# Convolution, attention and expert layers in one launch: a second convolution's split, copies and bursts moved between VectorE, ScalarE and GpSimd

## The chip, the core and the metric

The kernel runs on one core of one Trainium2 chip. A core has five engines that run side by side, each in the order of its own instruction stream: TensorE (PE; its weight loads are listed apart as PEld), VectorE (DVE), ScalarE (ACT), GpSimd (POOL) and SyncE (SP), which here only issues DMAs. They wait for each other through semaphores. The metric is the device time of one launch in microseconds (us), the median of several runs; lower is better.

## The reference

The input is x, 8 images of 56 x 56 positions with 256 channels, float32. Two layers follow each other:

```
# layer 0: 32 narrow paths, each 256 -> 4 -> 4 (3x3) -> 256, summed
h = relu(bn(x @ w1 + b1))            # per path, D = 4
h = relu(bn(conv3x3(h, w2) + b2))
h = relu(bn(h @ w3 + b3))
x = relu(paths.sum(axis=0) + x)
# layer 1: linear attention over an image's tokens, then experts
t = tokens(x)                                    # (8, 3136, 256)
q = ln(t); k = layernorm_per_head(q); v = layernorm_per_head(q)   # 8 heads of 32
kv = einsum('bhnd,bhne->bhde', k, v) / N
t = t + (einsum('bhnd,bhde->bhne', q, kv) + q)
u = ln(t); top2 = top_k(softmax(u @ router_w.T), 2)
t = t + (u + sum over the two experts of weight * expert(u))   # gelu(u @ w1 + b1) @ w2 + b2
```

The layer norms of the heads use the unbiased standard deviation plus 1e-5. The weights of the two experts are normed to the sum 1.

## The kernel before

**Chunks and slots.** The tokens are cut into S = 56 chunks of 448 tokens (CH), seven for each image. The main loop (L1395) runs over slots s = 0 to 64. A slot holds work on several chunks at once: the third convolution of chunk s (`conv3_steps`), the first of chunk s + 2, the second of chunk s + 1, the attention sums of chunk s - 1 (`end_steps`), the attention output of chunk s - 8 (`attn_steps`), the routing of one or two earlier chunks (`route_steps`), the planning of expert tiles (`plan_steps`), and expert tiles of 256 rows (`moe_steps`). Slots 0 to 8 have convolutions and sums alone, later ones attention too, then experts; the slots after 56 have no convolution, and the last expert tiles run by themselves.

**Order.** Every kind of work is a list of steps, pairs of a cost and a function. `issue` (L1368) lays each list over a stretch of the slot, for instance 0.12 to 1.0 for `end_steps`: a step stands at the middle of its share of the cost, and all steps of the slot are issued by position. The costs are thus only spacing. On PE, ACT and DVE this order is the engine's order; POOL and SP get theirs from a scheduler at build time, and it is fixed as well.

**Third convolution.** `pair` (L577) is the pulse of the kernel: two matmuls into two PSUM tiles (L587), a ReLU on ACT from the first into `r` (L592), and one DVE instruction that takes the maximum of the second and adds `r` (L595). A chunk has 32 pairs. After each four, `sum_paths` (L601) adds the four `r` with matmuls (L608). PSUM has seven working tiles, `r` seven buffers.

**Second convolution.** `conv2_steps` (L289) makes 24 small matmuls in three steps; ACT writes `h2` (L306). The next step, `halves` (L309), splits it for the products of pairs: DVE rounds `h2` to `hi` (L314) and takes the rest, `lo` (L315), and SP spreads both with 16 DMAs of 56 KB into `hl` (L320), in four groups (`ab`) of hi, lo, hi, lo. The first four pairs of the next slot read group 0, the next four group 1, and so on.

**Sums for the heads.** In `end_steps`: DVE sums each head's 32 channels (`means`, L667) and scales the result (L670), POOL subtracts it from the tokens (`center`, L681), ACT squares (L690), DVE works out the variances in one step (L699 to L718), POOL raises 36 numbers a partition to the power 0.5 (L719), DVE inverts (`inverse`, L727 to L733), POOL multiplies (L737), PE makes the products (L747).

**Attention, routing, experts.** `attend` (L866) has two matmuls, an update of X on DVE (L874) and statistics (L881, L882); after the fourth, POOL takes a power -0.5 of four numbers a partition (L885), and `means` (L887) uses it on DVE (L889) and `normed` on ACT (L894). `rows` (L1011) writes the two weights and the token's number behind the 256 values of each row of `pay` (L1019 to L1021); POOL scatters the rows to a region in DRAM (L1031). `take_rows` loads 256 of them into `z` (tag "rows", four buffers), `take_weights` an expert's weights (L1234, four buffers). `tile_in` (L1239) turns `z` and copies its weights to `g` (L1252) and its numbers to `index` (L1256); `tile_out` (L1295) scales the product by `g` on ACT (L1311), and POOL adds the result into the output by a scatter (L1325).

Of the kernel before, what the change touches and what calls it, by code (L numbers as in the profile page):

```python
# [8 lines left out]
F32 = mybir.dt.float32  # L9
BF16 = mybir.dt.bfloat16  # L10
I32 = mybir.dt.int32
F32R = mybir.dt.float32r
# [13 lines left out]
def kernel(  # L26
# [24 lines left out]
    nc = tc.nc  # L51
# [174 lines left out]
    nc.gpsimd.memset(h1[:, 1 : HW + 1, HW + 1 : W58], 0.0)  # L226

    def is_chunk(s):
        return 0 <= s < S
# [59 lines left out]
    def conv2_steps(s):  # L289
        ps = []  # L290

        def taps_of(dy):
            if dy == 0:
                ps.append(ps_mm.tile([P, 512], F32, tag="mm", name=f"c2_{s}"))
            R = tapped[s]
            for g in range(NG):
                nc.tensor.matmul(  # L297
                    ps[0][32 * g : 32 * g + 32, :CH],
                    W2t[:, g, dy, :],
                    R[:, g, :].rearrange("q (r w) -> q r w", w=W58)[:, dy : dy + ROWS, :HW],  # L300
                    start=(dy == 0), stop=(dy == 2),
                )
            if dy == 2:
                del tapped[s]
                h2 = split.tile([P, CH], F32, tag="h2", name=f"h2_{s}")
                nc.scalar.activation(h2, ps[0][:, :CH], AF.Relu, bias=sh2, scale=sc2)  # L306
                h2s[s] = h2

        def halves():  # L309

            h2 = h2s[s]
            hi = split.tile([P, CH], F32R, tag="hi", name=f"hi_{s}")
            lo = split.tile([P, CH], F32R, tag="lo", name=f"lo_{s}")
            nc.vector.tensor_copy(hi, h2)  # L314
            nc.vector.tensor_tensor(lo, h2, hi.bitcast(F32), ALU.subtract)  # L315
            hl = hlp.tile([P, NQ, CH], F32R, tag="hl", name=f"hl_{s}")
            for ab in range(NQ):
                for v, part in enumerate((hi, lo, hi, lo)):
                    queue = nc.scalar if s == 0 and v % 2 else nc.sync
                    queue.dma_start(  # L320
                        out=hl[v : P : 4, ab, :].bitcast(F32),
                        in_=part[32 * ab : 32 * ab + 32, :].bitcast(F32),
                    )
            h2s[s] = hl

        return [
            (0.8, lambda: taps_of(0)), (0.8, lambda: taps_of(1)), (0.8, lambda: taps_of(2)),
            (0.8, halves),
        ]

# [75 lines left out]
    for f in range(NF):  # L406
        tp = ps_mm.tile([P, 512], F32, tag="mm", name=f"tp_sb_{f}")
        nc.tensor.transpose(tp[:, :NP], bias3[:, f * P : (f + 1) * P], ident[:NP, :NP])
        b3T = setup.tile([P, NP], F32, name=f"b3T_{f}")
        nc.scalar.copy(b3T, tp[:, :NP])  # L410
        sub = setup.tile([P, NQ, NPL], F32, name=f"sub_{f}")
        nc.vector.tensor_copy(
            sub, b3T.rearrange("q (a r n) -> q a r n", r=2, n=NPL)[:, :, 1, :]
        )
        nc.vector.tensor_reduce(
            sumb[:, f, :], sub.rearrange("q a n -> q (a n)"), AX.X, ALU.add
        )
    setup_pool.__exit__(None, None, None)

# [65 lines left out]
    Wd = tc.dram_tile([E, P, WROW], F32, name="Wd")  # L485

    b2hl = const.tile([P, C], F32R, name="b2hl")
    b2s = const.tile([P, C], F32, name="b2s")
    b2l = const.tile([E, C], F32R, name="b2l")
    nc.gpsimd.memset(b2s, 0.0)  # L490
    nc.sync.dma_start(out=b2s[:E], in_=b2)
    nc.vector.tensor_copy(b2hl, b2s)
    nc.vector.tensor_tensor(b2l, b2s[:E], b2hl[:E].bitcast(F32), ALU.subtract)
    nc.sync.dma_start(out=b2hl[E : 2 * E].bitcast(F32), in_=b2l.bitcast(F32))
    pos_i = const.tile([P, 2], I32, name="pos_i")
# [9 lines left out]

    ids = const.tile([T, KT], I32, name="ids")
    nc.gpsimd.iota(ids, [[T, KT]], base=0, channel_multiplier=1)
    def tiles_after(n):
# [127 lines left out]
    def end_steps(s):  # L636
# [28 lines left out]
        def means():  # L665
            m = v["m"] = small([T, KT, NH], "hmean")
            nc.vector.tensor_reduce(  # L667
                m, v["t"].rearrange("q k (h c) -> q (k h) c", c=HC), AX.X, ALU.add
            )
            nc.vector.tensor_scalar_mul(m, m, 1.0 / HC)  # L670

# [6 lines left out]

        def center():
            for f, n in enumerate(heads(norm)):  # L680
                nc.gpsimd.tensor_tensor(  # L681
# [13 lines left out]
        def variances():  # L695

            sd = v["sd"] = small([T, KT, NH + 1], "hsd")
            ss = small([T, KT, NH], "hss")
            nc.vector.tensor_reduce(  # L699
                ss, v["sq"].rearrange("q k (h c) -> q (k h) c", c=HC), AX.X, ALU.add  # L700
            )
            m = v["m"]
# [5 lines left out]
                op0=ALU.mult, op1=ALU.add,  # L708
            )
            nc.vector.tensor_mul(dm, dm, dm)  # L710
            nc.vector.scalar_tensor_tensor(
                dm, dm, float(HC), ss, op0=ALU.mult, op1=ALU.add
            )
            nc.vector.tensor_reduce(mu, dm, AX.X, ALU.add)
            nc.vector.tensor_scalar(
# [7 lines left out]
        def inverse():  # L723
# [6 lines left out]
            )  # L730
            nc.vector.reciprocal(inv, inv)
            rs1s[s] = keep.tile([T, KT], F32, tag="rs1", name=f"rs1_{s}")
            nc.vector.reciprocal(rs1s[s], sd[:, :, NH])  # L733
# [8 lines left out]
        def products():  # L742
# [13 lines left out]

        return [
            (0.1, begin), (0.6, lambda: turn(0)), (0.6, lambda: turn(1)), (0.6, means),
            (1.0, center), (0.6, squares), (1.8, variances), (0.8, inverse), (0.8, scale),
            (1.9, products),  # L760
        ]
# [91 lines left out]
    def attn_steps(a):  # L853
# [9 lines left out]
        nm = stat.tile([T, KT], F32, tag="nm", name=f"nm_{a}")  # L863
        late = []

        def attend(k):  # L866
# [10 lines left out]
            )  # L877
            late.append(lambda: nc.scalar.copy(lg[:, k, :], ps[:, C:]))
            if k:
                late.pop(0)()  # L880
            nc.vector.bn_stats(st[:, k, :], X[:, k, :])  # L881
# [5 lines left out]
        def means():  # L887
            late.pop(0)()
            nc.vector.scalar_tensor_tensor(  # L889
                nm, mv[:, :, 0], -1.0, rs2, op0=ALU.mult, op1=ALU.mult  # L890
            )

# [6 lines left out]
        def base():  # L899
# [9 lines left out]

        return (  # L910
            [(1.0, lambda k=k: attend(k)) for k in range(KT)]
            + [(0.6, means)]
            + [(0.4, lambda k=k: normed(k)) for k in range(KT)]
            + [(0.6, base)]
        )
# [11 lines left out]
    def route_steps(group):  # L927
# [10 lines left out]
        def logit():  # L938
            lg = v["lg"] = small([E], "rlg")
            for n, m in enumerate(group):  # L940
# [4 lines left out]
                )  # L945
                nc.vector.tensor_add(mine, mine, raw[:, :, E:])

        dsc = desc[:T, None, :].to_broadcast([T, K, E])

        def wide(t):  # L950
            return t[:, :, None].to_broadcast([T, K, E])

        def best(n):
# [10 lines left out]
            nc.vector.tensor_reduce(mx, lg, AX.X, ALU.max)  # L964
            nc.vector.tensor_tensor(sel, lg, wide(mx), ALU.is_equal)
            nc.vector.tensor_tensor(sel, sel, dsc, ALU.mult)
            nc.vector.tensor_reduce(at, sel, AX.X, ALU.max)
            nc.vector.tensor_tensor(sel, dsc, wide(at), ALU.is_equal)

        def weights():  # L970
            q = v["q"] = small([], "rq")
            nc.vector.tensor_sub(q, v["mx", 1], v["mx", 0])
            for n, m in enumerate(group):
                mine = q[:, n * KT : (n + 1) * KT]
                nc.vector.tensor_mul(mine, mine, pays[m][3])  # L975
            nc.gpsimd.tensor_tensor(q, ebase[:T, :K], q, ALU.pow)  # L976
            both = v["both"] = small([2, E], "rboth", BF16)
            nc.vector.tensor_copy(both, v["sel"])
# [32 lines left out]
        def rows():  # L1011
            q2 = v["q"]
            q1 = small([], "rq1")
            nc.vector.tensor_scalar_add(q1, q2, 1.0)
            nc.vector.reciprocal(q1, q1)
            for n, m in enumerate(group):
                pay = pays[m][0]
                mine = slice(n * KT, (n + 1) * KT)
                nc.vector.tensor_copy(pay[:, :, C], q1[:, mine])  # L1019
                nc.vector.tensor_mul(pay[:, :, C + 1], q2[:, mine], q1[:, mine])  # L1020
                nc.vector.tensor_scalar_add(pay[:, :, C + 2].bitcast(I32), ids, m * CH)  # L1021
            row = small([2], "rrowf")
# [7 lines left out]
        def scatter(n, m, k):  # L1030
# [12 lines left out]

        return [
            (0.5, logit), (0.5, lambda: best(0)), (0.5, lambda: best(1)), (0.5, weights),
            (0.6, ranks), (0.5, rows),
        ], [
# [162 lines left out]
    def empty_rows(e):  # L1210
        pad = slots.tile([P, 2, ROW], F32, tag="rows", name=f"pad_{e}")
        nc.gpsimd.memset(pad, 0.0)
# [7 lines left out]
    def take_rows(i):  # L1220
        row = entry(i, 0, E * CAPR - TR)
        z = slots.tile([P, 2, ROW], F32, tag="rows", name=f"rows_{i}")
        region = regions[slot_of[i][2]]
# [15 lines left out]
    def tile_in(i):  # L1239
# [9 lines left out]
        nc.scalar.copy(eT, tp)  # L1249

        g = slots.tile([P, 2], F32, tag="g", name=f"g_{i}")
        nc.vector.tensor_copy(g, z[:, :, C + k])  # L1252
        index = slots.tile([P, 2], I32, tag="index", name=f"index_{i}", bufs=6)
# [250 lines left out]
```

## Time and profile before

| | |
|---|---|
| median of 3 runs | 3389.59 us (3385.21 to 3398.8) |
| the profiled execution's own time | 3376.6 us |
| its span, first to last instruction | 3374.9 us |
| mean granted TensorE clock | 0.951 |
| PE busy | 3001.6 us, 89% |
| DVE busy | 2179.8 us, 65% |
| ACT busy | 1895.8 us, 56% |
| POOL busy | 1928.4 us, 57% |
| DMA | 537.72 MB, mean 159 GB/s |

Busy time is the time in which an engine executed something. A group of the profile gives line, engine, operation, output <- input, shape and count, and then busy time, mean duration in ns, the engine's idle time just before, and what ended most of it. In the timeline each row has the start, the duration and the instruction; a bracket is the idle time of that engine before it, with the instruction that ended it. Rows that follow each other with equal work are merged, with a count. Executions differ a little: the profiled one lies 13 us under the median.

### The profile page before, as it was taken

The numbers are of one execution on the slowest core, as the hardware profiler recorded it, in microseconds if no ns is written. First come the engines' busy times: TensorE is split into PE (matmuls) and PEld (weight loads), VectorE is DVE, ScalarE is ACT, GpSimd is POOL, SyncE is SP. The second block draws the span as 40 slices with busy tenths as digits, with TensorE's granted clock in tenths as the row PEclk, the third lists the DMA queues.
The fourth block names the chain that finished last, engine by engine and source line by source line (L and its number), as shares of the span: only waits on it lengthen the run. The fifth ranks groups of instructions, "written<-read, shape, count | busy, mean of one in ns | idle before, by whom it ended". The sixth has DMA issues, their size and how long they took to land. (4 is left out here: it accounts for less than half of the span.)

```text
span 3374.9 us, 55166 instructions
## 1 busy us (share of the span) xinstructions
PE 3001.6 (89%) x16677; PEld 1697.5 (50%) x16677; DVE 2179.8 (65%) x5762; ACT 1895.8 (56%) x3799; POOL 1928.4 (57%) x1386
## 2 busy tenths in 40 slices
PE   5888888888898999999999999899989987888698
PEld 2343433443444554555545555455444545676577
DVE  3666777777877777776776777776777774333200
ACT  2656555545565666566655666566656654443345
POOL 2222244444556566657565666746656657777677
PEclk7999989989999999999999999999999999988799
DMA  6432334445466676666666667567665756888797
GB/s 146 121 86 84 91 103 123 120 123 150 129 162 159 164 197 168 166 165 174 175 163 163 159 185 187 148 177 187 158 180 152 187 149 159 201 217 218 173 222 178
DMA packets 341481, 537.72 MB, mean 159 GB/s; under 512 B 59952, under 2 KB 251584, under 8 KB 341184
## 3 DMA queue, kind: packets, MB, share of 16 engines
q1 hardware_dynamic: 257088, 429.93, 43.8%
q0 software_dynamic: 81984, 103.45, 16.9%
q8 instruction: 134, 2.20, 0.3%
q14 instruction: 163, 1.34, 0.1%
q10 hardware_dynamic: 2112, 0.81, 0.1%
HBM read 248.01 MB, written 192.55 MB: 131 GB/s over the span
## 5 line engine op out<-in xcount | busy, mean ns | idle before, releaser
L595 DVE SCALAR_TENSOR_TENSOR r<-c,nb,r 128x448 f32<-128x448 f32 x1792 | 1127.3, 676 | 556.7 <-ACT r L592 482.8
L592 ACT ACTIVATE r<-c,b3t 128x448 f32<-128x448 f32 x1792 | 1033.2, 636 | 359.4 <-PE c L587 338.6
L1325 POOL DMA_INDIRECT out_dram<-y,index x420 | 662.8, 1578 | 356.3 <-ACT y L1311 243.7
L587 PE MATMUL c<-hl,W3hl 64*128 64x448 f32 x3584 | 708.4, 428 | 74.4 <-ACT r L592 37.7
L608 PE MATMUL su<-r,gather 128*32 128x448 f32 x3584 | 574.5, 568 | 64.9 <-DVE r L595 38.4
L1031 POOL DMA_INDIRECT regions<-pay,rrowi x448 | 433.1, 967 | 314.1 <-PE c L587 204.2
L587 PEld LDWEIGHTS c<-hl,W3hl 64*128 64x128 f32 x3584 | 341.9, 188 | 505.6 <-issue 227.1
L1287 PE MATMUL ph<-eT,w 128*128 128x256 f32 x1680 | 468.1, 410 | 55.7 <-DMA w<-Wd 23.8
L1307 PE MATMUL py<-w,hT 128*128 128x256 f32 x1680 | 435.6, 384 | 0.0
L1311 ACT ACTIVATE y<-py,g 128x256 f32<-128x256 f32 x420 | 196.7, 475 | 402.1 <-PE py L1307 303.1
L1287 PEld LDWEIGHTS ph<-eT,w 128*128 128x128 f32 x1680 | 306.9, 198 | 196.9 <-issue 101.8
L719 POOL TENSOR_TENSOR hsd<-hsd,half 112x36 f32<-112x36 f32 x56 | 351.7, 6280 | 78.4 <-DVE hsd L718 77.7
L1291 ACT ACTIVATE hT<-ph,w 128x256 f32<-128x256 f32 x420 | 198.1, 477 | 308.5 <-PE ph L1287 165.6
L1307 PEld LDWEIGHTS py<-w,hT 128*128 128x128 f32 x1680 | 293.9, 193 | 28.7
L681 POOL TENSOR_TENSOR norm<-t,hmean 112x512 f32<-112x512 f32 x112 | 120.2, 1130 | 322.1 <-PE c L587 175.0
L870 PE MATMUL at<-tab,tT 128*112 128x272 f32 x896 | 266.1, 421 | 11.9 <-ACT y L1311 6.8
L608 PEld LDWEIGHTS su<-r,gather 128*32 128x32 f32 x3584 | 104.2, 110 | 272.9 <-issue 135.5
L1303 PE MATMUL py<-b2hl,own 128*128 128x256 f32 x420 | 178.7, 425 | 22.4 <-ACT pay L894 8.1
L870 PEld LDWEIGHTS at<-tab,tT 128*112 128x112 f32 x896 | 149.4, 181 | 92.0 <-issue 17.3
L297 PE MATMUL c<-R,W2t 96*32 96x448 f32 x1344 | 180.1, 567 | 3.9 <-DMA R<-h 3.0
L894 ACT ACTIVATE pay<-X,nm,rs 112x256 f32<-112x256 f32 x224 | 134.9, 603 | 75.1 <-DVE nm L889 64.4
L976 POOL TENSOR_TENSOR rq<-ebase,rq 112x8 f32<-112x8 f32 (+1 forms) x32 | 52.9, 1654 | 197.0 <-DVE rq L975 197.0
(246 smaller groups left out, 3198.5 us busy)
## 6 DMA issues: line engine op xcount, KB each, us to landing
w<-Wd SPq DMA_DIRECT2D x210, 513.0 KB
rows<-regions SPq DMA_DIRECT2D x210, 259.0 KB
xi<-in_x_dram SPq DMA_DIRECT2D x56, 448.0 KB
hl<-hi SPq DMA_DIRECT2D x448, 56.0 KB
tTs<-u SPq DMA_DIRECT2D x56, 448.0 KB
ts<-t SPq DMA_DIRECT2D x56, 448.0 KB
tT<-tTs SPq DMA_DIRECT2D x56, 448.0 KB
X<-ts SPq DMA_DIRECT2D x56, 448.0 KB
```

Source lines behind the costliest of these rows:

```text
L587: product = nc.tensor.matmul(tiles[g][:, :CH], W3hl[rows, ab, cg, :], hl[rows, ab, :], start=True, stop=True)
L592: nc.scalar.activation(r, tiles[0][:, :CH], AF.Relu, bias=b3t[:, cg, 2 * ab : 2 * ab + 1])
L595: nc.vector.scalar_tensor_tensor(r, tiles[1][:, :CH], nb3[:, cg, 2 * ab + 1 : 2 * ab + 2], r, op0=ALU.max, op1=ALU.add,)
L608: nc.tensor.matmul(ps[32 * c4 : 32 * c4 + 32, :CH], gather, unit.pop((s, 4 * u + c4)), start=(ab == 0), stop=(ab == NQ - 1),)
L719: nc.gpsimd.tensor_tensor(sd, sd, half[:T, :].rearrange("q (k h) -> q k h", k=KT), ALU.pow)
L870: nc.tensor.matmul(ps, tT[:, f, k * T : (k + 1) * T], tables_of[b][:, f, :], start=(f == 0), stop=(f == NF - 1),)
L1031: ins = nc.gpsimd.indirect_dma_start(out=regions[n], out_offset=bass.IndirectOffsetOnAxis(ap=v["row_i"][:, (m - group[0]) * KT + k, n : n ...
L1287: nc.tensor.matmul(ps, w[:, f * C + hf * P : f * C + (hf + 1) * P], eT[:, f, :], start=(f == 0), stop=(f == NF - 1),)
L1291: nc.scalar.activation(hT[:, hf, :], ps, AF.Gelu, bias=w[:, 2 * NF * C + hf : 2 * NF * C + hf + 1])
L1307: nc.tensor.matmul(ps, hT[:, f, h * P : (h + 1) * P], w[:, (NF + f) * C : (NF + f + 1) * C], start=False, stop=(f == NF - 1),)
L1311: nc.scalar.activation(y[:, h, :], ps, AF.Identity, scale=g[:, h : h + 1])
L1325: ins = nc.gpsimd.indirect_dma_start(out=out_rows, out_offset=at, in_=y[:, h, :], in_offset=None, compute_op=ALU.add, **partial,).ins
```

## The change

- `conv2_steps`: ACT writes both `h2` and `hi` from PSUM; DVE's rounding copy goes. `lo` is made by POOL instead of DVE.
- `end_steps`: the two large sums over heads are each made in two halves, and the chain of the variances is cut over five steps, that of the inverse over two. `in_parts` runs a function as a generator, one part for each step. The scaling by 1/32 goes from DVE to ACT, at the head of `center`. A step without work, `pause`, of cost 1.7 stands between the power and the inverse, and one of 0.3 behind the inverse; the cost given to the variances goes from 1.8 to 1.2.
- `attn_steps`: each `attend` is cut in two, and pauses stand on both sides of `means`; the token's number is written by an iota on POOL in a step of its own.
- `route_steps`: the steps are cut in parts; `rows` takes the reciprocal straight into `pay`, without copies, and adds no numbers; q + 1 is an instruction with two tensors.
- Expert tiles: `g` is now a view of `z`, so that `z` is held until `tile_out`; `z` has five buffers instead of four.
- The preparation of `b2hl` moves into the setup pool, which frees its memory; `ids` goes.

The core of the diff:

```
+    def in_parts(cost, n, fn):
+        run = []
+        def part(k):
+            if not run:
+                run.append(fn())
+            for _ in run[0]:
+                if k < n - 1:
+                    return
+        return [(cost / n, lambda k=k: part(k)) for k in range(n)]
+    def pause(cost):
+        return (cost, lambda: None)
...
-                nc.scalar.activation(h2, ps[0][:, :CH], AF.Relu, bias=sh2, scale=sc2)
-                h2s[s] = h2
+                hi = split.tile([P, CH], F32R, tag="hi", name=f"hi_{s}")
+                for part in (h2, hi):
+                    nc.scalar.activation(part, ps[0][:, :CH], AF.Relu, bias=sh2, scale=sc2)
+                h2s[s] = (h2, hi)
...
-            nc.vector.tensor_copy(hi, h2)
-            nc.vector.tensor_tensor(lo, h2, hi.bitcast(F32), ALU.subtract)
+            nc.gpsimd.tensor_tensor(lo, h2, hi.bitcast(F32), ALU.subtract)
...
-            nc.vector.tensor_reduce(
-                m, v["t"].rearrange("q k (h c) -> q (k h) c", c=HC), AX.X, ALU.add
-            )
-            nc.vector.tensor_scalar_mul(m, m, 1.0 / HC)
+            for h in range(2):
+                nc.vector.tensor_reduce(
+                    m[:, 2 * h : 2 * h + 2],
+                    v["t"][:, 2 * h : 2 * h + 2].rearrange("q k (h c) -> q k h c", c=HC),
+                    AX.X, ALU.add,
+                )
+                yield
...
         def center():
+            nc.scalar.mul(v["m"], v["m"], 1.0 / HC)
...
-            (0.1, begin), (0.6, lambda: turn(0)), (0.6, lambda: turn(1)), (0.6, means),
-            (1.0, center), (0.6, squares), (1.8, variances), (0.8, inverse), (0.8, scale),
-            (1.9, products),
+            (0.1, begin), (0.6, lambda: turn(0)), (0.6, lambda: turn(1)),
+            *in_parts(0.8, 2, means), (1.0, center), (0.6, squares),
+            *in_parts(1.2, 5, variances), pause(1.7), *in_parts(0.5, 2, inverse), pause(0.3),
+            (0.8, scale), (1.9, products),
...
+        def number():
+            nc.gpsimd.iota(
+                pay[:, :, C + 2].bitcast(I32), [[T, KT]], base=a * CH, channel_multiplier=1
+            )
...
-            [(1.0, lambda k=k: attend(k)) for k in range(KT)]
-            + [(0.6, means)]
+            sum((in_parts(1.0, 2, lambda k=k: attend(k)) for k in range(KT)), [])
+            + [pause(0.6), (0.3, means), pause(0.2)]
             + [(0.4, lambda k=k: normed(k)) for k in range(KT)]
-            + [(0.6, base)]
+            + [(0.1, number), (0.5, base)]
...
-            nc.vector.tensor_scalar_add(q1, q2, 1.0)
-            nc.vector.reciprocal(q1, q1)
+            nc.vector.scalar_tensor_tensor(
+                q1, q2, 1.0, half[:T, :K], op0=ALU.add, op1=ALU.max
+            )
...
-                nc.vector.tensor_copy(pay[:, :, C], q1[:, mine])
-                nc.vector.tensor_mul(pay[:, :, C + 1], q2[:, mine], q1[:, mine])
-                nc.vector.tensor_scalar_add(pay[:, :, C + 2].bitcast(I32), ids, m * CH)
+                nc.vector.reciprocal(pay[:, :, C], q1[:, mine])
+                nc.vector.tensor_mul(pay[:, :, C + 1], q2[:, mine], pay[:, :, C])
+                yield
...
-            (0.5, logit), (0.5, lambda: best(0)), (0.5, lambda: best(1)), (0.5, weights),
-            (0.6, ranks), (0.5, rows),
+            *in_parts(0.5, 2, logit), *in_parts(0.5, 2, lambda: best(0)),
+            *in_parts(0.5, 2, lambda: best(1)), *in_parts(0.5, 2, weights),
+            (0.6, ranks), *in_parts(0.5, 3, rows),
...
-        z = slots.tile([P, 2, ROW], F32, tag="rows", name=f"rows_{i}")
+        z = slots.tile([P, 2, ROW], F32, tag="rows", name=f"rows_{i}", bufs=5)
...
-        g = slots.tile([P, 2], F32, tag="g", name=f"g_{i}")
-        nc.vector.tensor_copy(g, z[:, :, C + k])
+        g = z[:, :, C + k]
```

## The prediction

> **What bounds the kernel now.** I began with the shares of the page and then asked for busy times in stretches of 150 us (columns: PE, PEld, DVE, ACT and POOL busy, clock, DMA share, GB/s).
>
> ```profile
> PE 3001.6 (89%) x16677; PEld 1697.5 (50%) x16677; DVE 2179.8 (65%) x5762; ACT 1895.8 (56%) x3799; POOL 1928.4 (57%) x1386
> ...
> 300.00:450.00 150.00, 128.63 (x713) 57.55 (x715) 111.53 (x242) 84.76 (x160) 45.14 (x23) 0.94 0.32 89
> 1500.00:1650.00 150.00, 144.81 (x857) 78.83 (x856) 107.59 (x284) 97.02 (x195) 90.29 (x61) 1.00 0.66 175
> 3000.00:3150.00 150.00, 114.11 (x566) 96.42 (x564) 46.17 (x227) 60.33 (x139) 112.81 (x85) 0.86 0.77 201
> ```
>
> PE sets the pace: no other engine is over 65%. So the time to be won is PE's idle time, 3374.9 - 3001.6 = 373 us. It is 14% before 900 us, 3 to 7% in the full slots after 1050 us, and 24% in the slots without convolution. I went through PE's timeline gap by gap and sorted the gaps by the DVE instructions in the 3 us before each. One form repeats in every slot of convolutions (period 37.8 us, from the starts of L262):
>
> ```profile
> 272.19 1.21 DVE L699 TENSOR_REDUCE hss<-sq 112x32 f32<-112x1024 f32 x1
> 274.51 0.17 DVE L718 TENSOR_SCALAR hsd<-hss 112x32 f32<-112x32 f32 x1
> 274.76 6.13 POOL L719 TENSOR_TENSOR hsd<-hsd,half 112x36 f32<-112x36 f32 x1 [6.69 <-DVE hsd L718]
> 277.56 0.38 DVE L314 CAST hi<-h 128x448 fp32r<-128x448 f32 x1
> 277.97 0.63 DVE L315 TENSOR_TENSOR lo<-h,hi 128x448 fp32r<-128x448 f32 x1
> 280.92 0.19 DVE L727 SCALAR_TENSOR_TENSOR hinv<-hsd 112x32 f32<-112x32 f32 x1 [2.32 <-POOL hsd L719]
> 281.46 2.42 DVE L595 SCALAR_TENSOR_TENSOR r<-c,nb,r 128x448 f32<-128x448 f32 x4
> 282.16 1.53 PE L608 MATMUL su<-r,gather 128*32 128x448 f32 x4 [2.25 <-DVE r L595]
> ```
>
> DVE stands at L727 until the 6.13 us power ends; the r behind it come late, and PE stands 2.25 us. The second form is in slots that route:
>
> ```profile
> 470.52 1.21 DVE L667 TENSOR_REDUCE hmean<-t 112x32 f32<-112x1024 f32 x1
> 472.12 2.05 POOL L681 TENSOR_TENSOR norm<-t,hmean 112x512 f32<-112x512 f32 x2 [4.75 <-PE c L587]
> 472.30 0.90 DVE L1019 COPY pay<-rq 112x4 f32<-112x4 f32 x1
> 473.18 1.02 DVE L1021 TENSOR_SCALAR pay<-ids 112x4 int32<-112x4 int32 x1
> 474.96 0.17 DVE L1028 CAST rrowi<-rrowf 112x16 int32<-112x16 f32 x1
> 475.78 2.29 PE L608 MATMUL su<-r,gather 128*32 128x448 f32 x4 [2.79 <-DVE r L595]
> ```
>
> From 470.52 to 475.04 DVE does no r, and two tiny copies take 0.90 and 1.02 us where others of their line take 0.16.
>
> The sums of PE's gaps: **A**, behind the inverse: 35.4 us in 16 gaps before 900 us, 18.5 in 20 after, 53.9. **B**, behind `rows`: 14.8 + 7.4 = 22.2. **C**, behind nm (L889): 2.4 + 5.3 = 7.6. **D**, behind the variances: 1.9. Not touched: the image steps (L781, L829; 41), the plan's bursts (13.6), the start, and most of the tail's 92 us. ACT's bursts hold PE too: 16.7 us behind the squares (L690) before 900 us.
>
> [...] L1019 and L1021 are stretched exactly under L681, while L595[...] keeps 650 to 687 ns throughout. [...] this trace has 1.05 us for 512 numbers a partition on POOL (L681) and 0.63 us for 448 on DVE (L315), so 1.5 times for each number. [...]
>
> **The change part by part**, against the span of 3374.9 us.
>
> *DVE.* Gone: hi 56 x 0.40 = 22.4, lo 35.0, the g copies 48.5, L1019 40.6, L1021 24.4, L670 11.4, together 182 us of its 2180. Added: each large sum in halves costs a second fixed part; from L705 (32 numbers, 0.176) and L699 (1024, 1.212) a half of 512 is 0.676, so 0.14 more for each of 112, 16 us. Nearly all of that 166 us lies beside PE's work and is worth nothing by itself; what counts is A to D.
>
> *A.* In the built order four r stand between the power's release and L727, before and after. So the pause moves nothing on DVE as such; what moves is the release. Before, the whole chain from L699 to L718 (272.19 to 274.68, 2.5 us) stands ahead of it; after, its sums come four r earlier and only three small instructions (0.55 us) are left. The release comes 2.5 - 0.55 = 1.9 us earlier against PE, the power ends earlier by as much, and hi and lo (1.0 us), which were hidden under the power, don't matter. Of a 2.25 us gap 0.3 to 0.4 us are left: 80% of 53.9, 43 us saved. In slots with attention rs (L885, 1.04 us) runs just ahead of the power in POOL's order and costs half a us of that.
>
> *B.* Before 4.5 us without r. After, in the built order, a run of some 15 small ones stands between two r: statistics 0.61, half a sum 0.68, L1014's successor 0.2, two reciprocals (L733: 0.12) and products (0.15), X 0.48, three of 0.22 to 0.29: 3.1 us. 1.4 of 2.8 goes, and some with the earlier start: 60%, 13 us. *C, D*: 3 us; the pause moves nm by 0.02 of a slot (1 us) only.
>
> *ACT.* hi costs 56 x 0.725 (L306) = 40.6, the scaling 56 x 0.17 (L878) = 10. The four r on ACT behind it come 0.73 late; in the slot shown ACT stood 1.34 us idle two r later, which hides it, and with experts ACT is at 97 of 150. Both ends: nothing, or 0.73 in each of 56 slots, 41 us, if no cover is there. I take 8. Against the squares the chain scaling, center, squares, L699 is now closer (squares to L699 0.027 of a slot, 1 us, where 1.16 us of squaring lie between): DVE may stand 0.5 us there, 3 us for all.
>
> *POOL.* lo: from L681 (512: 1.052) and L900 (1024: 2.188) 448 numbers take 0.91 us, 51 us in all; an iota (0.13) 7. The queue matters, not the sum: in POOL's order lo stands directly behind the 6.13 us power, with one to three scatters of 0.97 us between in later slots. In the slot shown the power would end near 279.2, lo near 280.3 instead of 278.6; its first four DMAs are issued by 282.8 (0.64 each), landed near 285 (the last of the slot is issued at 287.45 and the queue is empty near 289). The next slot's first pair, at 288.27 before, wants group 0 near 286. Slack 1 us at least; the later groups need 2.5 us of issue each and are used over 4 us. With experts the slot is 46 to 60 us and the slack over 4. Price taken: 0. SP stands at lo some 2 us longer in a slot; behind it wait the stores of X and the expert loads, which are needed two tiles (20 us) later.
>
> *Expert tiles.* `take_rows` now waits for the third last tile's L1311 instead of L1256 a tile earlier: rows come one tile (4.13 us at the end) later, and the weights behind them on SP about 1.8 us later (0.85 for L1311's two, 0.95 for the next load's issue). They still have 2 x 4.13 + 0.6 - 1.8 = 7.1 us. The DMA share there is 0.92 in 3150 to 3300 us, so landing may take 5. Bounds: -5 (no g copies stuck behind index) and +30 (1 us for each of 30 last tiles). Taken: 0.
>
> *Start.* lo of chunk 0 is behind POOL's eight pads; with five buffers the last pad moves from 57.8 to 51.7, so lo comes 1 us late: +1.
>
> Sum: -43 - 13 - 3 + 8 + 3 + 1 = **-47 us**, 3328 for the span. The profiled execution lies 13 us under the median, so for the median 3389.6 - 47 = **3342 us**.
>
> **Rivals.** *Same time*: with four r between, DVE reaches L727 one us sooner (hi and lo gone) and simply waits longer, if the release doesn't move because the squares are late. Then only B and C are won, 16, against 8 to 12 on ACT: 3385. For it: the unchanged count of r. Against it: L699 never waited for the squares before ("idle 0.0" in its group). *Slower*: lo comes too late, a new wait of PE for hl at each slot's start. It begins when lo ends over 1 us later than worked out, and decides once it is 47/56 = 0.84 us more than that; at 2 us more: 56 x 2 - 47 = +65, 3455; at 1.4 more +31, 3420. For it: up to three scatters wait for PE ahead of lo. Against it: only one wait for hl in the trace (8 us, at the start). *The tail pays*: the late rows cost their upper bound, 3372. The change does do what it says: the built order shows each move.
>
> **How the numbers follow.** Main case 0.63 (own range 3310 to 3372: with the ACT bound at 25, or with all of A and B won), same 0.15, tail pays 0.07, slower 0.15. Range 3300 to 3405: it leaves out most of the slower case and a gain of over 90, which would need all of A to D (85.6) and a part of ACT's gaps. A measurement of this kernel can tell about 0.5%, 17 us (3373 to 3406). Faster 0.68 (main, and half of the tail case), same 0.17, slower 0.15.
>
> **What would show it.** The period of L262 in slots of convolutions falls from 37.8 to near 35.7 us; L727's successor still waits for POOL, but PE's 2.25 us gap at L608 is under 0.6. The gap of 2.79 in routing slots is near 1.1. No PE wait for hl beyond the start. L1311 and the last tiles keep 4.13 us a tile. Wrong if: waits of PE for hl or of lo's DMAs appear each slot; L699's successor waits for the squares over 1 us; ACT's r hold PE more than 20 us longer than now; PE's waits for w in the tail grow from 23.8 us.

## The result, and the profile after

The changed kernel takes 3521.4 us (median of four runs, 3518.7 to 3526.3), the kernel before 3387.8 in the same comparison: 1.039 times as long, 95% interval 1.036 to 1.042. The forecast was 3342 with a range of 3300 to 3405. It is wrong, and on the wrong side. The profiled executions differ by 3518.6 - 3374.9 = 143.7 us.

The page of the changed kernel, its line of busy times, and the same stretches of 150 us as before (columns: PE, PEld, DVE, ACT and POOL busy, clock, DMA share, GB/s):

```profile
PE 3110.3 (88%) x16677; PEld 1772.2 (50%) x16677; DVE 2154.4 (61%) x5408; ACT 1938.2 (55%) x3911; POOL 1993.5 (57%) x1497
...
300.00:450.00 150.00, 130.19 (x702) 61.96 (x701) 100.91 (x212) 83.64 (x157) 37.22 (x21) 0.91 0.31 88
1500.00:1650.00 150.00, 139.48 (x781) 76.27 (x780) 103.20 (x243) 90.47 (x184) 89.05 (x64) 0.98 0.58 150
3000.00:3150.00 150.00, 118.34 (x570) 98.03 (x569) 49.52 (x214) 57.63 (x134) 119.01 (x87) 0.88 0.81 197
```

PE executes the same 16677 matmuls, yet it is recorded as busy for 109 us longer. In 150 us of full slots it gets through 781 instead of 857 of them. So most of the loss isn't recorded as idle time of PE, but as matmuls that last longer. A timeline of the same form of slot as before (convolutions alone, from 231.5 us) shows the first reason. The changed kernel has other line numbers: its L602 and L607 are L587 and L592 of the kernel before, L610 is L595, L623 is L608.

```profile
244.76 0.17 DVE L743 TENSOR_SCALAR hsd<-hss 112x32 f32<-112x32 f32 x1
...
245.01 6.12 POOL L744 TENSOR_TENSOR hsd<-hsd,half 112x36 f32<-112x36 f32 x1 [6.10 <-DVE hsd L743]
...
251.10 1.13 POOL L332 TENSOR_TENSOR lo<-h,hi 128x448 fp32r<-128x448 f32 x1
251.17 1.10 DVE L752 SCALAR_TENSOR_TENSOR hinv<-hsd 112x32 f32<-112x32 f32 x1 [2.03 <-POOL hsd L744]
...
252.62 2.43 DVE L610 SCALAR_TENSOR_TENSOR r<-c,nb,r 128x448 f32<-128x448 f32 x4
...
253.32 1.60 PE L623 MATMUL su<-r,gather 128*32 128x448 f32 x4 [2.78 <-DVE r L610]
...
256.99 3.81 PE L773 MATMUL kv<-norm 112*128 112x129 f32 x16
```

Lo starts the moment the power ends and runs beside hinv. Hinv, 0.19 us before, takes 1.10 and ends with lo. The gap of PE that was to shrink from 2.25 to 0.3 us has grown to 2.78. The sixteen matmuls of kv behind it take 3.81 us, where the kernel before has

```profile
285.43 2.02 PE L747 MATMUL kv<-norm 112*128 112x129 f32 x16
```

The granted clock is 0.50 there, from 254.66 us on for 6.83 us; in the slot shown of the kernel before it stays at 1.00.

The second reason is in full slots. PE's timeline shows it, first in the kernel before and then in the changed one:

```profile
1477.42 0.67 PE L587 MATMUL c<-hl,W3hl 64*128 64x448 f32 x4
1478.03 1.17 PE L870 MATMUL at<-tab,tT 128*112 128x272 f32 x4
1479.13 0.69 PE L587 MATMUL c<-hl,W3hl 64*128 64x448 f32 x4
```

```profile
1370.03 0.88 PE L602 MATMUL c<-hl,W3hl 64*128 64x448 f32 x5
1371.22 1.18 PE L602 MATMUL c<-hl,W3hl 64*128 64x448 f32 x3 [0.31 <-ACT r L607]
```

Before, the products of attend (at) stand between two groups of four partial convolutions. After, they have moved ahead, and eight partial convolutions follow one another: 2.4 us from 1370.03 to the end, where two separate fours take 1.36. PE waits there for ScalarE's r to free one of the seven PSUM tiles (`ps_mm`), and most of that wait is counted as busy: of the 1.0 us more, 0.31 stand as idle. The waits of PE's weight loads give the sums (us, times, longest), before and after:

```profile
PEld c L587 <- ACT r L592: 156.1, 288, 3.0
...
PEld su L608 <- DVE r L595: 103.9, 142, 3.6
```

```profile
PEld c L602 <- ACT r L607: 223.8, 483, 6.1
...
PEld su L623 <- DVE r L610: 149.1, 181, 3.8
```

PE's order is fixed when the kernel is built, and the traces have it: 132 runs of eight partial convolutions before, 205 after (the rest are runs of four).

### The profile page after: what moved, and what is told of

Its sections match the earlier page's. It is cut to its first block, busy times and chain, and to the rows that moved or that the text cites. A ratio compares the mean times of both kernels' runs of the same rounds, so it can differ in the third digit from the quotient of the medians.

```text
span 3518.6 us, 55086 instructions
## 1 busy us (share of the span) xinstructions
PE 3110.3 (88%) x16677; PEld 1772.2 (50%) x16677; DVE 2154.4 (61%) x5408; ACT 1938.2 (55%) x3911; POOL 1993.5 (57%) x1497
## 4 chain that ended last, share of the span: by engine, by line
PE 49%; issue 11%; POOL 10%; ACT 8%; DVE 7%; DMA 3%; SPq 1%; POOLq 0%; another core or an unknown queue 0%; ACTq 0%; DVEq 0%
PE ph L1320 9%; PE su L623 8%; PE py L1340 7%; PE c L602 7%; POOL hsd L744 5%; PE at L896 5%; ACT r L607 4%; PE kv L773 3%; DVE r L610 2%; PE c L276 2%; POOL out_dram L1358 2%; PE te L1280 2%; PE py L1336 2%; POOL regions L1065 2%; PE tu L670 2%
## 5 line engine op out<-in xcount | busy, mean ns | idle before, releaser
L610 DVE SCALAR_TENSOR_TENSOR r<-c,nb,r 128x448 f32<-128x448 f32 x1792 | 1130.2, 677 | 589.7 <-ACT r L607 501.0
L607 ACT ACTIVATE r<-c,b3t 128x448 f32<-128x448 f32 x1792 | 1027.8, 636 | 339.5 <-PE c L602 324.8
L602 PE MATMUL c<-hl,W3hl 64*128 64x448 f32 x3584 | 794.1, 436 | 94.3 <-ACT r L607 44.0
L602 PEld LDWEIGHTS c<-hl,W3hl 64*128 64x128 f32 x3584 | 383.5, 191 | 569.9 <-ACT r L607 223.8
L623 PE MATMUL su<-r,gather 128*32 128x448 f32 x3584 | 580.5, 586 | 66.8 <-DVE r L610 66.5
L1320 PE MATMUL ph<-eT,w 128*128 128x256 f32 x1680 | 471.4, 412 | 38.1 <-DMA w<-Wd 13.8
L1340 PE MATMUL py<-w,hT 128*128 128x256 f32 x1680 | 444.2, 390 | 0.0
L1344 ACT ACTIVATE y<-py,rows 128x256 f32<-128x256 f32 x420 | 196.9, 475 | 407.4 <-PE py L1340 269.1
L896 PE MATMUL at<-tab,tT 128*112 128x272 f32 x896 | 258.7, 412 | 0.7 <-ACT y L1344 0.7
L623 PEld LDWEIGHTS su<-r,gather 128*32 128x32 f32 x3584 | 106.1, 111 | 258.0 <-DVE r L610 149.1
L1336 PE MATMUL py<-b2hl,own 128*128 128x256 f32 x420 | 188.5, 449 | 31.5 <-DVE nm L913 18.1
L900 DVE SCALAR_TENSOR_TENSOR X<-at,rs,X 112x256 f32<-112x256 f32 x224 | 107.5, 480 | 121.2 <-PE at L896 103.2
L1280 PE MATMUL te<-ident,rows 128*128 128x128 f32 x840 | 136.2, 286 | 49.2 <-DMA rows<-regions 38.8
```

The source lines that it names most:

```text
L602: product = nc.tensor.matmul(tiles[g][:, :CH], W3hl[rows, ab, cg, :], hl[rows, ab, :], start=True, stop=True)
L607: nc.scalar.activation(r, tiles[0][:, :CH], AF.Relu, bias=b3t[:, cg, 2 * ab : 2 * ab + 1])
L610: nc.vector.scalar_tensor_tensor(r, tiles[1][:, :CH], nb3[:, cg, 2 * ab + 1 : 2 * ab + 2], r, op0=ALU.max, op1=ALU.add,)
L623: nc.tensor.matmul(ps[32 * c4 : 32 * c4 + 32, :CH], gather, unit.pop((s, 4 * u + c4)), start=(ab == 0), stop=(ab == NQ - 1),)
L896: nc.tensor.matmul(ps, tT[:, f, k * T : (k + 1) * T], tables_of[b][:, f, :], start=(f == 0), stop=(f == NF - 1),)
L1280: nc.tensor.transpose(tp[:, f, h * P : (h + 1) * P], z[:, h, f * P : (f + 1) * P], ident)
```

## The experiments

Two theories came out of this. **Order**: cutting attend in two moves its products ahead, so that they no longer part the groups of partial convolutions. **GpSimd**: lo behind the power stretches hinv (0.19 to 1.10 us) and drops the clock (to 0.50). Two more causes were possible: the chunk's end in parts with its pauses, and the routing and the tiles. The time (us) is split here by stage of the profiled executions, from the starts of the first convolution's activation (L262, in the changed kernel L279): 2nd to 10th chunk (convolutions alone), 10th to 22nd (routing begins), 22nd to 56th (full slots). Each run was compared with the kernel before, whose medians lay between 3378 and 3389 us; so a difference between two runs of different groups is good to some 10 us.

| kernel | 2nd to 10th | 10th to 22nd | 22nd to 56th |
|---|---|---|---|
| before | 314.2 | 549.1 | 1789.0 |
| changed | 328.5 | 566.8 | 1890.8 |
| attention steps alone (f1) | 311.1 | 560.7 | 1889.0 |
| second convolution alone (f2) | 329.9 | 574.3 | 1812.1 |
| routing and tiles alone (f4) | 320.7 | 555.9 | 1789.7 |
| window of attention moved (g1) | 313.2 | 550.8 | 1878.2 |
| inverse and products later (h1) | 298.2 | 539.3 | 1764.8 |

**Parts undone, from the changed kernel.** In e1 lo goes back to VectorE, in e2 the attention steps, in e3 the chunk's end; e4 is e1 with e2.

```diff
# e1, e4
-            nc.gpsimd.tensor_tensor(lo, h2, hi.bitcast(F32), ALU.subtract)
+            nc.vector.tensor_tensor(lo, h2, hi.bitcast(F32), ALU.subtract)
# e2, e4 (and `late`, which delays ScalarE's copies of lg by a step, as before; the change had dropped it)
-            sum((in_parts(1.0, 2, lambda k=k: attend(k)) for k in range(KT)), [])
-            + [pause(0.6), (0.3, means), pause(0.2)]
+            [(1.0, lambda k=k: attend(k)) for k in range(KT)]
+            + [(0.6, means)]
# e3: means, variances, inverse whole, scaling on VectorE, no pauses, costs as before
```

> The changed kernel with one instruction back on VectorE: lo is computed by VectorE (0.63 us each) in place of GpSimd (1.12 us, directly behind the 6.13 us power). Order theory (attend in two parts lets eight partial convolutions run back to back on TensorE; that is most of the loss): the order of TensorE is the same as in the changed kernel, so most of the loss stays, 3490 to 3515 us. GpSimd theory ([...]hinv takes 1.10 us in place of 0.19, the gap of TensorE grows from 2.25 to 2.78 us and the clock halves behind it, in all 56 slots): hinv is back at 0.19 us, the slots of convolutions at 37 to 38 us, and 60 us or more come back, 3460 us or less.

> The changed kernel with the attention steps planned as before: attend whole, the copies of lg one step late, means at 0.6 without pauses; the iota stays. Runs of eight partial convolutions in TensorE's order fall from 205 to the 132 of the kernel before. Order theory: TensorE's waits of partial convolutions for the r of ScalarE fall from 224 us to near 156, and the time by 80 to 110 us, to 3410 to 3440. GpSimd theory: the slots without attention are untouched and the others keep their stretched hinv, so at most 30 us come back, over 3490.

> The changed kernel with the steps at a chunk's end as before: means and variances whole, the scaling of hmean on VectorE, no pauses around inverse; lo stays on GpSimd, attend in two. Order theory: TensorE's runs of eight stay at 205, so 3500 to 3530. Theory of the chunk's end (ScalarE waits 54 us for hmean, the pause moves the work on): 40 us or more come back, 3480 or less.

> The changed kernel with both: lo on VectorE and the attention steps as before. If order and GpSimd together are the whole loss, and what is left (hi on ScalarE, sums in parts, pauses, fewer copies, rows in parts) gains what was forecast for it less the cost on ScalarE, 3355 to 3390. If a third cause is open, over 3400.

Measured: e1 3479.8 us (1.0281 of before, 1.0246 to 1.0315), 42 less than the changed kernel; e2 3459.3 (1.0221), 62 less; e3 3543.0 (1.0462), 22 more; e4 3408.3 (1.0064, 1.0042 to 1.0086), 113 less. The expectations of e1 and e2 gave each theory a range, and both times fell between the two: both theories hold, neither alone carries the loss, and together they are 113 of 134. E4 lies over its 3400, so something smaller is open. In e1 hinv is back at 0.19 us in all 56 places (the expectation had it stretched in all of them; in the changed kernel it is so in 17) and five of six slots of convolutions take 37.1 us. In e2 the c waits for ScalarE fall from 223.8 to 169.4, in e1 they stay at 220.7. The chunk's end in parts was not a cause: without it the kernel is slower.

**One part alone, from the kernel before.**

```diff
# f1: attn_steps of the changed kernel (without the iota)
# f2: conv2_steps of the changed kernel (hi on ScalarE, lo on GpSimd)
# f4: all but conv2_steps, attend/means and end_steps
# e5: f4 with the changed end_steps
```

> The kernel before with one part of the change alone: the attention steps (attend in two parts, the copies of lg without delay, pauses around means). Order theory: TensorE's order gets 205 runs of eight partial convolutions in place of 132, its waits of partial convolutions for the r of ScalarE rise from 156 to 205 to 225 us, and the time by 60 to 110 us: 3445 to 3495. If the order hurts only together with the later lo, the time is within 20 us of the kernel before, 3370 to 3405.

> The kernel before with one part of the change alone: hi on ScalarE and lo on GpSimd. GpSimd theory: hinv grows from 0.19 to 1.1 us in most slots, the slots of convolutions take 38 to 41 us with a lower clock, 20 to 60 us slower than before: 3405 to 3445. If what costs is only lo behind a release that comes earlier (the new plan of the chunk's end), it is within 10 us of the kernel before.

> The changed kernel with three parts undone: the second convolution's copies, the attention steps and the chunk's end as before. What is left is routing in parts with fewer copies, the iota on GpSimd, the expert tiles without the g copies and with rows in five buffers. The forecast gave this part 13 us (the 2.79 us gap at the rows shrinks to 1.1): 3365 to 3380. If later rows in the expert tiles (waits of 17 to 39 us for rows) cost more than that, 3390 to 3410.

> The changed kernel with two parts undone: hi and lo on VectorE, and the attention steps as before; the chunk's end in parts with its pauses stays. Against the changed kernel with lo on VectorE and the attention steps as before (3408 us) only hi moves, from ScalarE to VectorE. If hi on ScalarE is what is left of the loss (0.72 us in each of 56 slots, 40 us at most): 3355 to 3380, below the kernel before. If it was hidden, 3400 to 3415, and the rest of the loss lies in the chunk's end or the tiles.

Measured: f1 3486.0 (1.0304, 1.0282 to 1.0326), 103 over before; f2 3436.2 (1.0152), 53 over; f4 3398.5 (1.0054, 1.0038 to 1.0070), 15 over; e5 3396.9 (1.0039). So the attention steps cost by themselves, as the order theory has it, nearly all of it in full slots; the second convolution costs most before them. F4 missed its forecast of a gain, and e5 lies between its two ranges: what is left of the loss there lies in the parts it shares with f4. Against e4, e5 has only hi on VectorE again: 1.0064 against 1.0039, 8 us, and the two intervals overlap. In f2, with the chunk's end as before, hinv is stretched in the same way (27 of 56 take over 0.5 us):

```profile
251.06 1.13 POOL L315 TENSOR_TENSOR lo<-h,hi 128x448 fp32r<-128x448 f32 x1
251.13 1.10 DVE L727 SCALAR_TENSOR_TENSOR hinv<-hsd 112x32 f32<-112x32 f32 x1 [2.75 <-POOL hsd L719]
...
253.28 2.29 PE L608 MATMUL su<-r,gather 128*32 128x448 f32 x4 [3.16 <-DVE r L595]
```

F4 shows a third, small cause. Its third chunk starts 5.8 us late, as in the changed kernel. ScalarE's first r at the start, before and after:

```profile
64.41 1.16 ACT L592 ACTIVATE r<-c,b3t 128x448 f32<-128x448 f32 x2 [0.84 <-DMA hl<-hi]
```

```profile
70.54 1.16 ACT L607 ACTIVATE r<-c,b3t 128x448 f32<-128x448 f32 x2 [7.16 <-DMA b2hl<-b2l]
```

The first r waits for the transfer of b2l. The change took b2s and b2l out of `const` into the setup pool, whose space the later tiles take over, so the first r seems to have to wait until this copy has been read. No run undoes this alone; but the third chunk starts at 76.5 to 79.2 us in all ten traces that have this part, and at 71.4 to 75.5 us in all eight that don't.

**The order by itself.** Two kernels move the attention steps' window only. G1 is the kernel before; g2 is e1, with attend still in two parts.

```diff
# g1
-            work_of.append((0.35 if opens else 0.05, 0.97, attn_steps(a)))
+            work_of.append((0.35 if opens else 0.08, 0.97, attn_steps(a)))
# g2 (on e1)
+            work_of.append((0.35 if opens else 0.1, 0.99, attn_steps(a)))
```

> The kernel before with one number altered: the attention steps' window starts at 0.08 of a slot in place of 0.05. Nothing is cut, moved to another engine or added; TensorE's order alone gets 209 runs of eight partial convolutions in place of 132. Order theory: 60 to 110 us slower than before, 3445 to 3495. If it is the cutting of attend (its shorter parts on VectorE and ScalarE) that costs, within 15 us of the kernel before.

> The changed kernel with lo on VectorE (3480 us) and with attend still in two parts, but the attention steps' window at 0.10 to 0.99 in place of 0.05 to 0.97: the products of attend then stand between the partial convolutions again, 117 runs of eight in place of 205. Order theory: 60 us or more come back, 3380 to 3420. If the cutting itself costs: over 3450.

Measured: g1 3464.8 (1.0274, 1.0252 to 1.0296), 87 us over before by one number; g2 3378.5 (1.0002, 0.9990 to 1.0013), some 100 under e1. The cut of attend is harmless, its place is not. One slot in g1, from 1493.5 to 1541.6, is 2.5 us longer than the same slot before (45.6), and PE's timeline has the pieces: three groups of eight that were fours with an at between them, two of them here,

```profile
1494.84 0.87 PE L587 MATMUL c<-hl,W3hl 64*128 64x448 f32 x5
1496.03 1.19 PE L587 MATMUL c<-hl,W3hl 64*128 64x448 f32 x3 [0.32 <-ACT r L592]
1497.16 1.17 PE L870 MATMUL at<-tab,tT 128*112 128x272 f32 x4
...
1500.71 2.32 PE L587 MATMUL c<-hl,W3hl 64*128 64x448 f32 x8
1502.97 1.17 PE L870 MATMUL at<-tab,tT 128*112 128x272 f32 x4
```

2.38, 2.32 and 1.70 us against 1.36 for two fours: 1.0 + 1.0 + 0.3 = 2.3 of the 2.5. In the run at 1500.71 the last two matmuls start at 1502.05 and 1502.57, each 0.05 us after the end of an r on ScalarE (1502.00, 1502.52): from there PE goes at ScalarE's pace, and since a matmul by itself is recorded with 0.46 us, hardly any of that shows as idle.

G1's number moves the attention steps on every engine, so it doesn't isolate PE's order. What shows of it directly is the busy time of the partial convolutions, 708.4 us before and 755.6 in g1: 47 of the 85 us between the profiled executions. Another 39 stand in PE's waits of su for VectorE's r (38.4 and 77.0 us), which may as well come from VectorE's own order; no run parts the two.

**What the pause could have done.** In the kernel before and in the changed one, four r of VectorE stand between the release of the power and hinv. G3 takes the kernel before and puts eight there; g4 adds the changed second convolution.

```diff
-            (0.6, squares), (1.8, variances), (0.8, inverse), (0.8, scale),
-            (1.9, products),
+            (0.6, squares), (1.8, variances), (1.2, lambda: None), (0.2, inverse), (0.4, scale),
+            (1.7, products),
```

> The kernel before with the inverse moved by 1.2 of 8.8 in the chunk's end (and products shortened by as much, so that the steps ahead of it stay): eight r of VectorE instead of four stand between the power's release and hinv. If TensorE's 2.25 us gap behind hinv (54 us in all) is what the pause was to take away, and it only needed more r in between, the gap goes and the slots of convolutions fall from 37.8 to 35.5 to 36.5 us: 3325 to 3360. If products then wait for norm instead (scaled 3 us later): 3375 to 3395.

> Hi on ScalarE and lo on GpSimd as in the kernel before with that part alone (3436 us), and the inverse later as in the run above. If lo costs through VectorE, which stands at hinv until lo has ended while TensorE waits for the r behind it, then with eight r ahead of hinv nothing waits for it: within 15 us of the run above. If lo costs through late hl, or ScalarE's second activation, the 53 us stay.

Measured: g3 3405.9 (1.0092, 1.0075 to 1.0109), g4 3459.4 (1.0247). The forecast of a gain fell, by the rival named beside it, and g3 is slower still than that rival's 3395. The wait of PE behind hinv in the kernel before, and the waits in g3:

```profile
PE su L608 <- DVE r L595: 38.4, 20, 2.8
```

```profile
PE kv L747 <- POOL norm L737: 81.5, 80, 5.2
...
PE su L608 <- DVE r L595: 14.7, 8, 2.8
```

The wait behind hinv is down from 38.4 to 14.7 us, and a new one of kv for norm, 81.5 us, has taken its place. G4 tells which way lo costs: though nothing waits behind hinv any more (16.2 us), it is 53 us over g3, and kv's wait grows to 111.7, by 30 of the 53. So the stretched hinv is one face of it; lo stands in GpSimd's queue between the power and the scaling, and delays whatever of that chain PE meets first. The other 23 us, which include hi on ScalarE, no run separates.

**Room behind the chain.** H1 to h5 move products to the slot's end as well. H2 has another window of attention; h3 is the changed kernel with lo on VectorE and three positions altered; h5 is the changed kernel with those three alone.

```diff
# h1, h2
+            (1.2, lambda: None), (0.2, inverse), (0.4, scale), (1.5, lambda: None), (0.2, products),
# h2: window 0.06 to 0.91
# h3, h5: window 0.1 to 0.99, and
+            *in_parts(1.2, 5, variances), pause(2.5), *in_parts(0.4, 2, inverse), (0.4, scale),
+            pause(1.7), (0.2, products),
```

> The kernel before with the inverse later (3406 us alone) and the products moved to the slot's end as well, at 0.98 of the chunk's steps. If the only thing that took back the gain of the later inverse was TensorE's wait of kv for norm (82 us in 80 waits), that wait falls under 15 us, TensorE's waits behind hinv stay near 15, and the time is 3310 to 3350. If the work was only moved and the next slot's start pays: 3375 to 3400.

> The same, and the attention steps' window at 0.06 to 0.91 in place of 0.05 to 0.97: 88 runs of eight partial convolutions in TensorE's order in place of 103. Order theory: at 1.1 to 1.3 us for each run of eight, 15 us less than the run above at most; nothing, if runs of eight cost only in slots with expert tiles, where there are hardly any left.

> The changed kernel with lo on VectorE and three positions altered: the attention steps' window (0.10 to 0.99), the inverse later (eight r of VectorE ahead of hinv) and the products last; 88 runs of eight. If positions, not the cutting and not the moved copies, decide: below the kernel before, 3310 to 3350. If the parts of the change bring nothing of their own, as the run above or up to 15 us slower.

> The changed kernel as it is, lo on GpSimd too, with only those three positions altered. If lo costs because GpSimd's chain power, lo, scale, kv is in front of TensorE, it is harmless once kv has room: within 12 us of the run above. If it costs by itself (late hl[...]), 40 to 55 us slower than the run above.

Measured: h1 3313.4 us (0.9771 of before, 0.9744 to 0.9798), faster than both kernels; h2 3384.9 (0.9983, 0.9973 to 0.9994); h3 3332.7 (0.9837); h5 3338.7 (0.9857, 0.9831 to 0.9883). H5 is the whole change with those positions altered: from 3.9% slower to 1.4% faster. It is 6 us over h3, within the noise, so lo on GpSimd is nearly free once hinv and kv stand later. H3 itself is 19 us over h1, a little more than the 15 named: with the positions right, the parts of the change seem to bring nothing of their own. H1's page, stretches and waits:

```profile
PE 2986.3 (90%) x16677; PEld 1685.7 (51%) x16677; DVE 2191.6 (66%) x5762; ACT 1898.3 (57%) x3799; POOL 1923.0 (58%) x1386
```

```profile
300.00:450.00 150.00, 135.50 (x778) 63.07 (x772) 117.93 (x267) 91.46 (x172) 46.87 (x23) 0.94 0.35 100
1500.00:1650.00 150.00, 146.46 (x856) 79.47 (x855) 110.37 (x270) 99.11 (x199) 100.80 (x70) 1.00 0.69 184
```

```profile
PE su L608 <- DVE r L595: 15.5, 8, 2.8
...
PE kv L747 <- POOL norm L737: 8.7, 14, 2.7
```

Both waits are all but gone; most slots of convolutions take 35 us where 37.8 stood. VectorE is busy for 66% of the span, the highest share of all kernels here: relieving it was not what was needed.

H2 contradicts a plain count. It has 88 runs of eight and h1 103, yet it is 71 us slower, where its expectation had it faster or the same. GpSimd's timeline shows one reason, first h2 and then the same stretch of h1:

```profile
1484.09 6.15 POOL L719 TENSOR_TENSOR hsd<-hsd,half 112x36 f32<-112x36 f32 x1
1490.43 1.59 POOL L1325 DMA_INDIRECT out_dram<-y,index  x1 [0.19 <-ACT hT L1291]
1492.54 2.19 POOL L900 TENSOR_TENSOR X<-X,pay 112x1024 f32<-112x1024 f32 x1 [0.52 <-ACT pay L894]
1495.31 2.06 POOL L737 TENSOR_TENSOR norm<-norm,hinv 112x512 f32<-112x512 f32 x2 [0.59 <-DVE rs L733]
```

```profile
1465.65 2.05 POOL L737 TENSOR_TENSOR norm<-norm,hinv 112x512 f32<-112x512 f32 x2 [1.02 <-DVE rs L733]
1467.66 2.19 POOL L900 TENSOR_TENSOR X<-X,pay 112x1024 f32<-112x1024 f32 x1
```

The earlier attention puts X (2.19 us) ahead of the scaling, where h1 has it behind; kv's wait for norm is 33.8 us in place of 8.7. That is 25 of the 71. PE's list of waits has more: su waits 21.3 us for nm (in h1 not at all) and 29.1 for r (15.5), at 15.2 for ScalarE's r (4.4), while c waits 13.4 less. These are readings; no run separates them.

## Why the prediction was wrong

**Not in the sum: the order of PE.** This is the step that failed, and the largest term. The prediction gave C and D, with the attention steps, a gain of 3 us, and looked at the built order on VectorE ("four r stand between") and at POOL's queue, never at what stands between the partial convolutions on PE. It called PE the bound, took PE's busy time as given and its 373 us of idle time as all that could move, and costed the change on the engines that are not the bound. The attention steps alone cost 103 us (f1), one number that only re-times them costs 87 (g1), and moved back they cost nothing (g2). That their place costs this is shown; that it costs by PE's order is shown for about half, in the busy time of the partial convolutions.

**A, -43.** The release of the power came earlier, but by half of what was worked out: 14.5 us after the slot's L262 before (274.76 - 260.27), 13.5 after (245.01 - 231.53). The end of hinv moved only from 20.8 to 20.7 us behind that L262, because hinv took 0.91 us longer. That hi and lo "don't matter" was true of the place they left: under the power, on VectorE, lo was free. Behind the power, on GpSimd, it was not. The observation that four r stand there before and after was right and should have weighed more: a pause without an r in it covers nothing. Eight r, and room for kv, are worth 76 us to the kernel before (h1). That cutting the chunk's end in parts helps stays unclear: whole again it costs the changed kernel 22 us (e3), but added to f4 it gives nothing clear (e5).

**POOL, lo: 0.** This was asked about hl only, and rightly answered: PE's waits for hl are one, of 11.0 us at the start, 8.0 before. The cost came by what is queued behind lo. The prediction had seen two operations of VectorE, L1019 and L1021, take 0.90 and 1.02 us beside a GpSimd one (L681), where others of their lines take 0.16, but used this only for what the change removes. The change itself puts such a pair side by side: hinv beside lo takes 1.10 to 1.12 us in the 17 of 56 places where the two overlap, and 0.18 to 0.19 in the other 39. What the two contend for, no run shows. Together with lo's place in the chain this is 42 us (e1), and with hi on ScalarE, added to the kernel before, 53 (f2). Its duration too was low: 0.91 estimated from the rows of 512 and 1024, 1.15 measured in the median.

**The clock** was in no term. Of the six slots of convolutions one had kv at 3.81 us before and four have it after; each such slot is 2.5 to 3 us longer. The clock of these four slots falls to 0.50 at 131.78, 213.70, 254.66 and 292.20 us, which are 24, 12 and 11 times 3.41 us apart. Behind gaps of 2.25 us (before) the clock fell in one slot of six, behind 2.5 to 2.8 us (changed) in four, and in f2, behind 2.4 to 3.2 us, in all six: kv takes 3.81 us in four of them, and in the other two the four su ahead of it take 2.29 and 2.19, where 1.53 stands at a clock of 1.00. The gap alone doesn't decide it: in h1 the clock fell in two of the six (eight su at 281.63 us take 1.72 in place of 0.96), which have no gap over 0.9 us. What does decide it, no run shows.

**B, -13.** The gap did as forecast: 2.79 us before, 1.1 named, 1.06 measured, in the slot shown here:

```profile
494.26 0.18 DVE L1053 RECIPROCAL pay<-rq 112x4 f32<-112x4 f32 x1
...
497.19 2.45 DVE L610 SCALAR_TENSOR_TENSOR r<-c,nb,r 128x448 f32<-128x448 f32 x4
...
497.92 2.29 PE L623 MATMUL su<-r,gather 128*32 128x448 f32 x4 [1.06 <-DVE r L610]
```

But the part alone gained nothing (f4: 15 us slower, 6 of them at the start), and PE's waits for VectorE's r were 62.8 us there against 38.4. What one gap gave was lost in others; which of the part's edits did that is open.

**Smaller terms.** ScalarE's hi, +8: 8, within the noise (e4 against e5). Squares, +3: VectorE stands 21 us there in 27 places, 0.8 us each. Expert tiles, 0 in bounds of -5 to 30: the stretch after the last L262 is 8.7 us longer (709.7 against 701.0), 2.4 in f4; waits for rows appeared (38.8 us), those for w fell (23.8 to 13.8). Start, +1: 5.5, most likely by a part of the change that the sum left out, the move of b2s and b2l.

**The rivals.** The slower one had the side and not the mechanism: it waited for late hl. Of the signs that were named, the period (38.1 to 41.1 in place of 35.7) and the gap at hinv told against the forecast. So did ScalarE's r, though only in the waits of PE's weight loads (68 us more) and not in those of its matmuls (37.7 and 44.0). Waits for hl, squares and w did not. In the chances, 0.63 and half of 0.07 make 0.67 for faster, not 0.68; nothing rests on it.

## What to carry to other kernels

When the steps of several streams are merged by position, cutting a step in two also moves what is inside it: count, in the built order of the engine that bounds the kernel, what stands between its bursts before and after, and do so for every stream that the change re-times. A pause behind a long operation is worth only the work that falls into it, and the chain after it (here power, scaling, products) must be given as much room as the pause took. An operation moved to an engine that is idle on average still joins a queue: price it by what waits behind it there, and by what will run beside it on VectorE (hinv beside lo: 1.10 us in place of 0.19).

## What the runs showed of the hardware

- A busy PE can hide its waits for free buffers: eight partial convolutions were recorded as busy for 2.32 us where two fours, parted by another product, took 1.36. Over the kernel PE's busy time varied from 2967 us (h5) to 3110 (changed) with the same 16677 matmuls.
- Slots of convolutions come in steps: 37.8 or 40.3 us before, with kv at 2.02 or 3.81 us and a slot clock of 1.00 or 0.92. In the traces before and after all falls of the clock (50 and 66) lie whole multiples of 3.41 us apart. A half microsecond more of a gap (2.25 to 2.78) showed as 2.5 us or more in some slots and as 0.3 us in others.
- A GpSimd subtraction of 448 numbers took 1.13 us, and a VectorE operation of 32 numbers that began 0.07 us later took 1.10, its end following lo's by 0.05 us. Its like took 0.19 us where no such subtraction ran beside it, and in all 56 places once VectorE made lo (e1).
